# Fourteen single buffers for x1, planes kept on the chip, gates further ahead: a change to layer 1 of a four-layer kernel

## Chip, cores and metric

The kernel runs on one core of a Trainium2 chip. The metric is the device time of one execution in microseconds; of several runs the median is given. PE, ACT, DVE and POOL are the tensor, scalar, vector and GpSimd engines, SP the engine whose queue issues most transfers.

## What is computed

The input x has shape 256 x 256 x 128 (65,536 points of 128 channels, 33.6 MB in float32). Four layers follow each other, each x = x + layer(groupnorm(x)). Layer 0 is an attention over rows, layer 2 a triangle product like layer 1 but with 128 channels, layer 3 a small convolution. The change lies in layer 1 and in the first loads of layer 2. Layer 1 is:

```
xn = groupnorm(x)                                  # 32 groups, statistics over all points
a  = sigmoid((xn@Wa1 + ba1) * (xn@Wa2 + ba2))      # 16 channels
b  = sigmoid((xn@Wb1 + bb1) * (xn@Wb2 + bb2))      # 16 channels
g  = sigmoid(xn@Wg + bg)                           # 128 channels
z  = einsum('ikc,jkc->ijc', a, b)                  # 16 products of 256 x 256 matrices
x  = x + g * (layernorm_over_16_channels(z)@Wz + bz)
```

## The kernel before, in words

Between stages x lies in device memory with channels as rows: x1T after layer 0, x2T after layer 1. It is cut into NSC = 32 tiles of 128 channels x SC = 2048 points, 1 MB each, 8 KB per partition. The list order1 (L769) takes the tiles as 0, 16, 1, 17, and so on. Each engine and each transfer queue runs its instructions in the order in which the code lists them (manual_schedule); a transfer issued by SP that has to wait holds up all that SP issues after it. On-chip memory is handed out as a stack of pools; a pool has named buffers, bufs of each name, used in turn, so that the first writer of a new tile waits for all users of the old one. Where one pool is closed and another opened, the new one takes the addresses of the old.

**Before layer 1.** Layer 0 has three pools, one above the other: p2e (L481; the buffers p2_e, six of 8 KB per partition, and p2_es, five of 4 KB), p2c with the 8 KB tile triT, and p2 (p2_x, p2_rb and more). When they are closed, x1 is opened in their place: KEEP = 10 buffers of 8 KB (L772), and the first eight tiles are loaded by SP (load1, L775 to L781). A flag is then computed, and all engines branch on it (L795): a second, general attention follows only if the flag is set, which it isn't here. After the branch come the norm's factors (L198 to L209 and L818 to L829).

**Projections (L833 to L875).** Per tile, PE multiplies with two 128 x 32 weights (L859), ACT and DVE form the product (L868, L869), ACT the sigmoid into one of five p3_ab buffers (L842), and the four quarters of 64 KB go to abD, two through POOL and two through SP (store3, L848), one tile later. Of x, tiles 0 to 9 of the list stay in x1; the others pass through five more buffers (xs1, MORE = 5), tile i+5 being loaded when tile i is multiplied.

**Triangle product (L887 to L942).** For each of 16 channels, PE turns a matrix (L1822), ACT copies it out (L1824), PE multiplies (L1833), DVE subtracts plane 0 (L922) and sums (L928), ACT squares (L924) and POOL sums the squares (L929). Each plane is stored to znD at once (L933), not normalised. A pair of channels is loaded into one of three buffers z_A and z_B, and list positions 10 to 14 of x1 are loaded again on the way (L936). At the end DVE and ACT form the inverse deviation, 128 x 512 (L938 to L942).

**Gating (L947 to L1044).** For each position i of the list, in this order: PE and ACT make the gate of position i+LEAD (gate4; four matmuls in two halves, each through one of two PSUM buffers p4_pg, then a sigmoid into one of four buffers p4_g); SP fetches planes for four positions (fetch_z, each fourth i), and for every four positions PE spreads the inverse deviation over the rows through a p4_pg buffer and DVE multiplies the planes by it (scale_z, L969 and L972); PE multiplies the planes with Wz (L1014, p4_pz); DVE adds the bias and multiplies the gate, in place (L1022); POOL adds the result to x (L1033), or DVE does for the six positions in by_dve (L1029); ACT squares and sums the tile of i-1 for the next norm (sum4, L992), SP stores tile i-1 to x2T (L1039) and loads into a freed buffer (L1042). LEAD is 2. The first three gates are made ahead of the loop.

**Layer 2 opens (L1053 to L1186).** The norm's factors are computed from the sums, then seven tiles of x2T are loaded by SP (load5, L1103), the first four are squared (L1108) and summed by PE (L1124), and the main products (L1167) follow. Its buffers p5_x lie in the pool p5.

The profile shows names without layer and digits: x for the x1 tiles, p_ab, z_A, z_z, p_z (fetched planes), p_pg, p_g, p_pz, p_rb (spread deviation), p_junk (squares), p_x (p5_x in layer 2, p2_x in layer 0), p_e and p_es.

Of the kernel before, what the change touches and what calls it, by code (L numbers as in the profile page):

```python
# [16 lines left out]
P = 128  # L17
N = 256
# [14 lines left out]
def kernel(ctx: ExitStack, tc: tile.TileContext, a: dict, out: bass.AP):  # L33
# [734 lines left out]

    order1 = [b + h * NSC // 2 for b in range(NSC // 2) for h in range(2)]  # L769
    KEEP, MORE, FIRST = 10, 5, 8  # L770
    x1_scope = ExitStack()
    x1_pool = x1_scope.enter_context(tc.tile_pool(name="x1", bufs=KEEP))  # L772
    xs = {}

    def load1(i, pool):  # L775
        s = order1[i]
        xs[s] = pool.tile([P, SC], F32, name=f"x1_{s}", tag="x1")
        nc.sync.dma_start(xs[s], x1T[:, s * SC : (s + 1) * SC])

    for i in range(FIRST):  # L780
        load1(i, x1_pool)  # L781
# [51 lines left out]
    with x1_scope, tc.tile_pool(name="xs1", bufs=MORE) as xs_pool:  # L833
        with tc.tile_pool(name="p3", bufs=3) as sb, tc.tile_pool(
# [17 lines left out]
            for i in range(FIRST, KEEP + MORE):  # L852
                load1(i, x1_pool if i < KEEP else xs_pool)
            for i, s in enumerate(order1):
# [8 lines left out]
                if i >= KEEP and i + MORE < NSC:  # L863
                    load1(i + MORE, xs_pool)
# [12 lines left out]
        with tc.tile_pool(name="zc", bufs=1) as zc:  # L877
            s1 = zc.tile([P, 2 * N], F32, name="z_s1")

            spread = zc.tile([P, 16, 32], F32, name="spread")  # L880
            for h in range(2):
                nc.gpsimd.tensor_copy(
                    spread[:, :, 16 * h : 16 * h + 16],
                    sel[:, 16 * h : 16 * h + 16].unsqueeze(2).to_broadcast([P, 16, 16]),
                )

            with tc.tile_pool(name="z", bufs=2) as sb, tc.tile_pool(  # L887
                name="zps", bufs=3, space=PSUM
            ) as ps, tc.manual_schedule():
                s2 = sb.tile([P, 2 * N], F32, name="z_s2", bufs=1)  # L890
                base = sb.tile([P, 2 * N], F32, name="z_base", bufs=1)
                AB, stores = {}, []

                def load_z(g):
                    if g < 8:
                        AB[g] = [sb.tile([P, 2, 2 * N], F32, name=n, bufs=3) for n in ("z_A", "z_B")]
                        A, B = AB[g]
                        nc.sync.dma_start(A, abD[2 * g : 2 * g + 2, :].rearrange("c (p t) -> p c t", p=P))
                        for c in range(2):
                            nc.sync.dma_start(  # L900
                                B[:, c, :], abD[16 + 2 * g + c, :].rearrange("(q s t) -> s q t", q=4, t=CK)
                            )

                def turn_z(k):
                    if k < 16:
                        return tri_turn(nc, ps, sb, AB[k // 2][0], k % 2, ident, nc.scalar.copy)

                for g in range(3):
                    load_z(g)
                at = turn_z(0)  # L910
                for k in range(16):
                    if k and k % 2 == 0:
                        load_z(k // 2 + 2)
                    nxt = turn_z(k + 1)
                    pz = tri_multiply(nc, ps, at, AB[k // 2][1], k % 2).rearrange("p t n -> p (t n)")
                    at = nxt
                    Z = sb.tile([P, 2 * N], F32, name="z_z", bufs=4)
                    if k == 0:
                        nc.vector.tensor_copy(base, pz)
                        nc.vector.memset(Z, 0.0)  # L920
                    else:
                        nc.vector.tensor_tensor(Z, pz, base, ALU.subtract)  # L922
                        sq = s2 if k == 1 else sb.tile([P, 2 * N], F32, name="z_sq", bufs=3)
                        nc.scalar.activation(sq, Z, AF.Square)  # L924
                        if k == 1:
                            nc.vector.tensor_copy(s1, Z)
                        else:
                            nc.vector.tensor_tensor(s1, s1, Z, ALU.add)  # L928
                            (nc.vector if k == 15 else nc.gpsimd).tensor_tensor(s2, s2, sq, ALU.add)  # L929
                    stores.append((k, Z))  # L930
                    if len(stores) > 1 or k == 15:
                        for k_, Z_ in stores if k == 15 else stores[:1]:
                            nc.sync.dma_start(znD[k_].rearrange("(p t) -> p t", p=P), Z_)  # L933
                        stores = stores[1:]
                    if k % 2 == 1 and KEEP + k // 2 < KEEP + MORE:
                        load1(KEEP + k // 2, xs_pool)  # L936

                nc.vector.scalar_tensor_tensor(s1, s1, -1.0 / 16, s1, ALU.mult, ALU.mult)  # L938
                nc.vector.tensor_tensor(s2, s2, s1, ALU.add)
                nc.vector.tensor_scalar(s2, s2, 0.0, None, ALU.max)  # L940
                nc.scalar.activation(s2, s2, AF.Sqrt, bias=epst, scale=1.0 / 16)
                nc.vector.reciprocal(s1, s2)  # L942
# [4 lines left out]
            with tc.tile_pool(name="p4", bufs=3) as sb, tc.tile_pool(  # L947
                name="p4psg", bufs=2, space=PSUM
            ) as psg, tc.tile_pool(name="p4psz", bufs=2, space=PSUM) as psz, tc.manual_schedule():
                zs, gts, sums = {}, {}, []  # L950
                junk = sb.tile([P, SC], F32, name="p4_junk", bufs=1)
                by_dve = (5, 11, 17, 23, 29, NSC - 1)

                def fetch_z(i):
                    if i < NSC:
                        zs[i] = sb.tile([P, 2, CK], F32, name="p4_z")
                        for m in range(2):
                            nc.sync.dma_start(
                                zs[i][:, m, :],
                                znD.rearrange("k (j b t) -> b j k t", j=8, t=CK)[order1[i] + m],  # L960
                            )

                def scale_z(i):
                    if i < NSC:
                        rb = psg.tile([P, 2, CK], F32, name="p4_rb", tag="p4_pg")
                        for m in range(2):
                            for c in range(4):
                                q = slice(32 * c, 32 * c + 32)
                                nc.tensor.matmul(  # L969
                                    rb[q, m, :], lhsT=spread[q, order1[i] + m, :], rhs=s1[q, :], start=True, stop=True  # L970
                                )
                        nc.vector.tensor_tensor(zs[i], zs[i], rb, ALU.mult)  # L972

                def gate4(i):
                    if i < NSC:
                        xt = xs[order1[i]]
                        gts[i] = sb.tile([P, SC], F32, name="p4_g", bufs=4)
                        for h in range(2):
                            pg = psg.tile([P, 2, CK], F32, name="p4_pg")
                            for c in range(2):  # L980
                                k = 2 * h + c
                                nc.tensor.matmul(  # L982
                                    pg[:, c, :], lhsT=wgf, rhs=xt[:, k * CK : (k + 1) * CK], start=True, stop=True
                                )
                            nc.scalar.activation(
                                gts[i][:, h * 2 * CK : (h + 1) * 2 * CK], pg.rearrange("p c t -> p (c t)"),
                                AF.Sigmoid, bias=bgf,
                            )

                def sum4():  # L990
                    i = sums.pop(0)
                    nc.scalar.activation(  # L992
                        junk, xs[order1[i]], AF.Square, bias=c1neg, accum_out=qsum[:, i : i + 1]
                    )

                LEAD = 2
                fetch_z(0)
                fetch_z(4)
                for i in range(LEAD + 1):
                    gate4(i)  # L1000
                scale_z(0)
                for i, s in enumerate(order1):
                    xt = xs[s]
                    if i:
                        gate4(i + LEAD)
                    if i % 4 == 0:
                        fetch_z(i + 8)
                    if i % 4 == 2:
                        scale_z(i + 2)
# [25 lines left out]
                    if len(sums) > 1:  # L1035
                        sum4()
# [838 lines left out]
```

## Time and profile before

Three runs took 3423.06, 3427.47 and 3431.08 us; the profiled execution has a span of 3428.7 us.

| stretch of the profile | us from the start | length |
|---|---|---|
| layer 0 and before | 0 to 1481.7 | 1481.7 |
| first x1 loads, branch | 1481.7 to 1505.7 | 24.0 |
| norm factors, projections | 1505.7 to 1599.35 | 93.65 |
| triangle product, to the end of the reciprocal | 1599.35 to 1660.27 | 60.9 |
| gating, to its last add | 1660.27 to 1858.5 | 198.2 |
| layer 2 from its norm, layer 3 | 1858.5 to 3428.7 | 1570.2 |

Over the whole span PE is busy 92%, DVE 66%, ACT 59%, POOL 47%, and the x1 loads are 54 transfers of 1 MB. Such shares are means over stages with different limits, so a change in one stage has to be read in that stage: the table of windows gives busy times by stretch, the timeline what each instruction waited for ("[2.10 <-ACT p_g L985]" means that the engine stood idle for 2.10 us and that the sigmoid in L985 released it). A busy PE is not PE at its peak.

### The profile page before, as it was taken

To read this page: it belongs to the slowest core of one execution; us is meant where nothing else is said; L and a number is where in the kernel's file an instruction comes from. 1 tells how busy PE (TensorE), PEld (TensorE's weight loads), DVE (VectorE), ACT (ScalarE), POOL (GpSimd) and SP (SyncE) were. 2 spreads that over 40 slices of the span, in tenths; PEclk is the share of its full clock that TensorE was granted. 3 is DMA by queue.
4 is the path that set the end of the run, shared out by engine and by line. 5 is a ranking of instruction groups with operands and counts; after the bars stand their busy time and mean duration, and the time that the engine had idled before them with its cause. 6 is when DMAs were issued, how large, how long until landed. Compare 5 with 4: busy or idle time off the path is not lost.

```text
span 3428.7 us, 52984 instructions
## 1 busy us (share of the span) xinstructions
PE 3137.5 (92%) x20394; PEld 1652.5 (48%) x20394; DVE 2263.5 (66%) x2612; ACT 2015.2 (59%) x2204; POOL 1617.7 (47%) x928
## 2 busy tenths in 40 slices
PE   5769999999999999956896999999999999859998
PEld 5525555555555555513332444444899533324444
DVE  5627888888888888832454445544555677747876
ACT  3667777777777777623576444543444466736565
POOL 4146777777777777723364000000555344514443
PEclk8889999999999999979998999999999999969999
DMA  9882333333333333279595676856999899856764
GB/s 395 350 299 79 116 119 107 119 106 122 109 119 110 115 116 109 94 271 364 202 383 246 236 270 252 310 215 233 343 352 349 305 336 334 307 163 194 206 199 131
DMA packets 298860, 753.23 MB, mean 220 GB/s; under 512 B 75193, under 2 KB 145819, under 8 KB 249067
## 3 DMA queue, kind: packets, MB, share of 16 engines
q1 hardware_dynamic: 290571, 741.54, 59.8%
q0 software_dynamic: 7520, 6.67, 0.6%
q8 instruction: 163, 2.67, 0.3%
q10 hardware_dynamic: 512, 1.59, 0.1%
q14 instruction: 94, 0.77, 0.1%
HBM read 462.02 MB, written 287.66 MB: 219 GB/s over the span
## 4 chain that ended last, share of the span: by engine, by line
PE 42%; DMA 7%; POOL 2%; DVE 2%; issue 2%; ACT 1%; SPq 0%; ACTq 0%; POOLq 0%; DVEq 0%
PE p_pm L1167 13%; PE tp_z L1833 7%; PE p_pm L1320 6%; PE p_pm L1555 5%; PE tp_a L1822 2%; POOL x L1033 2%; DMA abD<-p_ab 2%; PE p_st L1124 1%; PE p_pt L1592 1%; DMA p_er<-eD 1%; PE p_eb L1081 1%; PE p_rz L1081 1%; DMA x<-x1T 1%; PE p_rk L1081 1%; PE p_pg L982 1%
## 5 line engine op out<-in xcount | busy, mean ns | idle before, releaser
L564 DVE TENSOR_TENSOR p_e<-p_S,triT 128x1024 f32<-128x1024 f32 x512 | 609.3, 1212 | 144.7 <-PE p_S L554 144.7
L574 POOL TENSOR_TENSOR p_es<-p_e 128x1024 f32<-128x1024 f32 x256 | 603.5, 2368 | 125.7 <-issue 66.1
L572 ACT ACTIVATE p_e<-p_e,mbT 128x1024 f32<-128x1024 f32 x512 | 552.0, 1138 | 61.4 <-DVE p_e L564 61.2
L1167 PE MATMUL p_pm<-p_zn,wf 128*128 128x512 f32 x1040 | 451.2, 596 | 1.4 <-DVE p_zn L1184 1.4
L539 PE MATMUL p_mm<-p_xn,w 128*128 128x512 f32 x768 | 405.0, 610 | 0.3 <-DVE p_v L534 0.3
L1167 PEld LDWEIGHTS p_pm<-p_zn,wf 128*128 128x128 f32 x1040 | 198.0, 191 | 255.4 <-issue 248.6
L554 PE MATMUL p_S<-p_q,p_k 32*128 32x256 f32 x4096 | 295.7, 401 | 3.5 <-DVE p_e L564 3.2
L554 PEld LDWEIGHTS p_S<-p_q,p_k 32*128 32x128 f32 x4096 | 186.2, 184 | 159.5 <-PE p_mm L530 91.7
L1569 POOL TENSOR_TENSOR p_q<-p_q,p_pb 128x2024 f32<-128x2024 f32 x32 | 144.1, 4502 | 250.9 <-DVE p_pb L1563 250.9
L1233 POOL DMA_DIRECT2D rs__18031<-rs2D x4 | 2.0, 500 | 533.2 <-PE p_pm L1167 533.2
L1833 PE MATMUL tp_z<-p_B,tp_at 128*128 128x256 f32 x1024 | 251.0, 388 | 2.6 <-DMA p_B<-bD 2.3
L587 PE MATMUL p_o<-p_e,p_v 128*32 128x256 f32 x4096 | 248.3, 383 | 0.0
L513 POOL TENSOR_TENSOR p_xn<-p_xn,p_rs 128x1024 f32<-128x1024 f32 x63 | 151.3, 2402 | 205.1 <-ACT p_xn L508 129.1
L1276 POOL TENSOR_TENSOR k<-k,p_sq 128x512 f32<-128x512 f32 x128 | 163.0, 1274 | 135.4 <-ACT p_sq L1274 135.4
L1386 POOL TENSOR_TENSOR p_x<-p_x,p_g 128x2048 f32<-128x2048 f32 x30 | 136.3, 4543 | 161.3 <-DVE p_g L1373 127.3
L1833 PEld LDWEIGHTS tp_z<-p_B,tp_at 128*128 128x128 f32 x1024 | 185.5, 191 | 25.5 <-issue 2.7
L539 PEld LDWEIGHTS p_mm<-p_xn,w 128*128 128x128 f32 x768 | 125.8, 190 | 104.4 <-issue 88.7
L1275 DVE TENSOR_TENSOR k<-tp_z,k 128x512 f32<-128x512 f32 x128 | 88.5, 692 | 129.4 <-ACT p_sq L1274 129.4
L587 PEld LDWEIGHTS p_o<-p_e,p_v 128*32 128x32 f32 x4096 | 120.2, 110 | 110.1 <-ACT p_g L545 41.5
L1272 ACT COPY p_K<-tp_z 128x512 f32<-128x512 f32 x128 | 75.0, 586 | 160.0 <-PE tp_z L1833 160.0
L545 ACT ACTIVATE p_g<-p_mm,bgh 128x512 f32<-128x512 f32 x128 | 88.0, 687 | 131.4 <-PE p_mm L539 131.3
L1200 DVE SCALAR_TENSOR_TENSOR p_b<-p_pm,b2w,p_b 128x1024 f32<-128x1024 f32 x64 | 82.1, 1284 | 125.0 <-PE p_pm L1167 110.6
(374 smaller groups left out, 5982.2 us busy)
## 6 DMA issues: line engine op xcount, KB each, us to landing
p_x<-x2T SPq DMA_DIRECT2D x64, 1024.0 KB
x<-x1T SPq DMA_DIRECT2D x54, 1024.0 KB
p_x<-in_x_dram SPq DMA_DIRECT2D x32, 1024.0 KB
p_x<-xT SPq DMA_DIRECT2D x64, 512.0 KB
x2T<-x SPq DMA_DIRECT2D x32, 1024.0 KB
aD<-p_a SPq DMA_DIRECT2D x32, 1024.0 KB
bD<-p_b SPq DMA_DIRECT2D x32, 1024.0 KB
p_A<-aD SPq DMA_DIRECT2D x32, 1024.0 KB
```

Of the source, the lines that this page charges most:

```text
L513: nc.gpsimd.tensor_tensor(xn, xn, groups[g]["rs"], ALU.mult)
L539: nc.tensor.matmul(pm, lhsT=w, rhs=t["xn"][:, cs_], start=True, stop=True)
L554: nc.tensor.matmul(Ss[h // 2][:, h % 2, u, :], lhsT=t["k"][hp, r * N + u * P : r * N + (u + 1) * P], rhs=t["q"][hp, r * N : (r + 1) * N], ...
L564: nc.vector.tensor_tensor(e[:, :, 2 * p : 2 * p + 2, :].rearrange("p u h n -> p h u n"), Ss[p], triT[:, 2 * p : 2 * p + 2, :, :], ALU.add,)
L572: nc.scalar.activation(e[:, u, :, :], e[:, u, :, :], AF.Exp, bias=mbT[:, u, i : i + 1])
L574: nc.gpsimd.tensor_tensor(es, e[:, 0, :, :], e[:, 1, :, :], ALU.add)
L587: nc.tensor.matmul(t["o"][hp, r % 2, :], lhsT=t["v"][:, r * 2 + u, hp], rhs=e[:, u, h, :], start=(u == 0), stop=(u == 1),)
L1167: nc.tensor.matmul(pm[:, c, :], lhsT=wf2[:, i, :], rhs=zns[s][:, k * CK : (k + 1) * CK], start=True, stop=True)
L1276: nc.gpsimd.tensor_tensor(k2, k2, sq, ALU.add)
L1320: nc.tensor.matmul(pm[:, c, :], lhsT=w, rhs=src[:, k * CK : (k + 1) * CK], start=True, stop=True)
L1555: nc.tensor.matmul(pm[:, 2 * c : 2 * c + 2, :], lhsT=w2c, rhs=src[:, r : r + 2, :], start=True, stop=True)
L1833: nc.tensor.matmul(pz[:, t, :], lhsT=at[:, u, t * P : (t + 1) * P], rhs=Bc[:, u, :], start=(u == 0), stop=(u == 1))
```

## The change

Line numbers in the text remain those of the kernel before. The change does this:

- x1 has fourteen pools of one 8 KB buffer each. In the projections tile i+14 of the list follows tile i in its buffer, so that positions 18 to 31 are left at the end. No x1 load is made in the triangle stage. The gating takes positions 24 to 31, 18 to 23 and then 0 to 17, and loads its own position j into the buffer of j-14: 18 loads instead of 17.
- The sixteen planes stay in one tile Z (32 KB per partition) in the pool z. After the reciprocal, DVE multiplies four planes at a time by the inverse deviation and SP stores them, 1 MB each. scale_z, spread and the stores inside the loop are gone. z_A and z_B have two buffers instead of three. In the steps ahead of the square root the same DVE operations stand in another order.
- LEAD is 4 instead of 2 and p4_g has five buffers instead of four; five gates are made ahead of the loop.
- The x tiles of layer 2 get a pool of their own, x5, opened ahead of p5 and so at lower addresses; the first four are loaded by POOL's queue.

```diff
-    KEEP, MORE, FIRST = 10, 5, 8
+    SLOTS, FIRST = 14, 8
...
-    x1_pool = x1_scope.enter_context(tc.tile_pool(name="x1", bufs=KEEP))
+    slots = [x1_scope.enter_context(tc.tile_pool(name=f"x1_{i}", bufs=1)) for i in range(SLOTS)]
...
-                if i >= KEEP and i + MORE < NSC:
-                    load1(i + MORE, xs_pool)
+                if i + SLOTS < NSC:
+                    load1(order1[i + SLOTS], i % SLOTS)
...
-                        AB[g] = [sb.tile([P, 2, 2 * N], F32, name=n, bufs=3) for n in ("z_A", "z_B")]
+                    AB[g] = A, B = [sb.tile([P, 2, 2 * N], F32, name=n) for n in ("z_A", "z_B")]
...
-                    if k % 2 == 1 and KEEP + k // 2 < KEEP + MORE:
-                        load1(KEEP + k // 2, xs_pool)
...
+            for q in range(4):
+                zq = Z[:, 4 * q : 4 * q + 4, :]
+                nc.vector.tensor_tensor(zq, zq, s1.unsqueeze(1).to_broadcast([P, 4, 2 * N]), ALU.mult)
+                nc.sync.dma_start(znD[4 * q : 4 * q + 4, :].rearrange("c (p t) -> p c t", p=P), zq)
...
+            order = [order1[i] for i in (*range(24, NSC), *range(18, 24), *range(18))]
...
-                        gts[i] = sb.tile([P, SC], F32, name="p4_g", bufs=4)
+                    gts[i] = sb.tile([P, SC], F32, name="p4_g", bufs=5)
...
-                LEAD = 2
+            LEAD = 4
...
-                    if i % 4 == 2:
-                        scale_z(i + 2)
...
-                    j = i - 3 + KEEP + MORE
+                j = i - 3 + SLOTS
...
-                        load1(j, x1_pool if j % (KEEP + MORE) < KEEP else xs_pool)
+                    load1(order[j], (j + 10) % SLOTS)
...
+    with tc.tile_pool(name="x5", bufs=7) as x5_pool, tc.tile_pool(name="p5", bufs=2) as sb, tc.tile_pool(name="p5psX", bufs=1, space=PSUM) as psX, tc.tile_pool(
-                xs[s] = sb.tile([P, SC], F32, name="p5_x", bufs=7)
-                nc.sync.dma_start(xs[s], x2T[:, s * SC : (s + 1) * SC])
+                xs[s] = x5_pool.tile([P, SC], F32, name="p5_x")
+                (nc.gpsimd if s < KB else nc.sync).dma_start(xs[s], x2T[:, s * SC : (s + 1) * SC])
```

## The prediction

> **What bounds the kernel now.** The change touches layer 1 and the first loads of layer 2. I read the table of windows first, cut where the stages of this part begin, then for each stage the timeline and the table of waits. Columns: stretch and its length, then busy time (and instructions) of PE, PEld, DVE, ACT and POOL, granted clock, DMA share, GB/s.
>
> ```profile
> 1464.00:1481.70 17.70, 7.51 (x12) 2.35 (x8) 12.03 (x16) 0.00 (x0) 4.10 (x2) 0.64 0.24 90
> 1481.70:1505.70 24.00, 1.12 (x4) 1.01 (x4) 0.81 (x6) 0.04 (x1) 0.00 (x0) 0.50 0.87 352
> 1505.70:1599.35 93.65, 63.68 (x532) 17.66 (x532) 25.56 (x41) 40.74 (x67) 31.57 (x64) 0.94 0.92 359
> 1599.35:1652.03 52.68, 42.71 (x192) 35.44 (x192) 20.29 (x30) 16.97 (x30) 16.14 (x15) 0.84 0.89 331
> 1652.03:1660.27 8.24, 3.71 (x9) 1.44 (x8) 7.25 (x7) 2.63 (x3) 1.09 (x1) 1.00 0.14 55
> 1660.27:1675.30 15.03, 11.04 (x32) 4.18 (x33) 1.22 (x1) 7.86 (x7) 0.00 (x0) 0.77 0.30 105
> 1675.30:1858.50 183.20, 161.84 (x600) 56.91 (x600) 101.62 (x148) 123.79 (x119) 117.67 (x26) 0.96 0.72 285
> ```
>
> Row 1: the tail of layer 0, DMA nearly idle. Row 2: nothing but the first eight x1 loads. Row 3, the projections: DMA. Row 4, the triangle product: DMA and PE by turns. Row 5: DVE's square root and reciprocal. Rows 6 and 7, the gating: no engine is full (PE 88%), so a chain sets the pace.
>
> Why row 2 is empty, from the waits of SP's queue and the timeline:
>
> ```profile
> SPq L778 <- DVE stats L638: 7.8, 1, 7.8
> ...
> 1463.50 0.64 PE L597 MATMUL p_z<-p_es,hot 128*32 128x256 f32 x8 [1.34 <-POOL p_es L574]
> ...
> 1505.66 1.28 ACT L207 ACT_TABLE_LOAD   x1 [44.70 <-SPq L795]
> ```
>
> The first x1 load writes what had been a p_e buffer, last used in 1464.1, yet waits for DVE's last reading of p_x, another pool. A pool here waits for every tile of each closed pool it overlaps. Behind the branch (L795) all wait for SP, and SP for the eight loads, until 1505.7.
>
> The gating, from the timeline (start, length, engine, line, what it had waited for):
>
> ```profile
> 1660.41 1.28 ACT L985 ACT_TABLE_LOAD   x1 [3.53 <-DVE z_s L942]
> ...
> 1686.88 3.05 PE L969 MATMUL p_rb<-z_s,spread 32*32 32x512 f32 x16 [2.10 <-ACT p_g L985]
> ...
> 1701.91 3.70 PE L982 MATMUL p_pg<-x,wgf 128*128 128x512 f32 x8 [0.99 <-ACT p_g L985]
> ...
> 1703.62 4.53 POOL L1033 TENSOR_TENSOR x<-x,p_g 128x2048 f32<-128x2048 f32 x1 [0.20 <-DVE p_g L1022]
> ```
>
> The first sigmoid waits for the last reader of the z pool (rule of pools again). The same matmuls took 3.05 after a wait of 2.10 and 1.92 at 1711.33 after one of 1.02: PE starts at half clock after a long wait.
>
> [...] waits of 2.10, 2.46 and 3.17 already brought it, waits up to 1.8 did not. [...]
>
> **The change part by part**, against the profiled span of 3428.7 (the three timed runs have a median of 3427.5). R is the end of the reciprocal, i a position of the gating loop.
>
> (1) *Fourteen single slots; projections.* Slots 0 to 7 take the first 64 KB above layer 0's small pool; the p2e pool (six 8 KB and five 4 KB buffers, 68 KB) lay there and was free at 1464.1. So the eight loads start then, not at 1481.7, and the branch opens when flag and loads are there, about 1491 (estimate: PE left the branch at 1489.8). From then the stage is DMA-bound: 32 tiles of 1.049 MB, 15 stores of 0.262 ahead of the last load, and 1.6 MB of layer 0's tail (17.7 us by 90 GB/s) are 39.1 MB; at 424 GB/s (the windows 1494 to 1500 had 423 and 426) 92.2 us, from 1466 (2 of latency) to 1558.3. I add 4 because SP's loads must follow layer 0's last small transfers through its queue (none to 14: the last x1T store landed at 1481.7). But a store now stands behind the load 17 tiles on, before it was 8: with five p_ab buffers the closing of tile m+5 waits for it, so 12 tiles are left after the last load, 12 x 1.75 (PE's 8 projection matmuls) = 21.0, and 3.3 from the last p_ab to the next stage, as now. End 1586.8 instead of 1599.35: **-12.5** (-20 to -6). Loads fall from 54 to 50; the five removed lie in the next stage, the one added in the gating.
>
> (2) *Triangle stage.* Five x1 loads and 16 plane stores go. PE repeats every 2.20 when nothing is late (1612 to 1618). The second multiply began 10.1 after the start; 13 x 2.20 to the fifteenth and 3.72 for the last two give 42.4 against 52.68: **-10.3** (-6 to -11). Two z_B buffers instead of three: a group's 1 MB is issued 4.9 before its use and lands in about 3.6, so it stays hidden. Row 5's DVE steps are the same ones in another order: 0. The memset of plane 0 lies ahead of the first multiply: 0.
>
> (3) *Planes normalised behind the last; start of the gating.* Four DVE multiplies 128x2048 at 2.29 and four 1 MB stores, each behind its multiply. 4.19 MB at some 360 GB/s (abD's 2 KB rows had 361 and 373) are 11.6; first issue R+2.6, landing 1.7: the last lands at R+15.9. Planes and gate buffers share an address range, so the first sigmoid waits for this store; behind it in ACT's queue stand all gates, and PE for PSUM. Then 1.28 table, 1.05 to PE's next half gate, four gates of 3.63 and 1.9 for the cold clock: first p_pz at R+34.6; now R+15.0: **+19.6** (+4 to +21; the low end if only the fetch of planes waited). Spread, scale_z and their eight p_z multiplies vanish.
>
> (4) *Pace of the gating.* Now scale_z costs eight times 1.92 of PE and a PSUM slot: stretches of six positions with two of them took 36 to 38, with one 32.5. Without it PE would need 3.63 + 1.07 = 4.70 per position. But gate i+4 goes into one of five buffers, and the fifth before it is gate i-1, which POOL reads until its add ends. With LEAD 2 and four buffers the same wait was for i-2. So a loop closes: POOL ends i-1, ACT +0.06 and 1.05, PE gate i+5 3.63 and p_pz of i+1, from its start to POOL 3.85, POOL's add 4.53: 13.12 for **two** positions. The by_dve positions are all odd and don't cut the even loop. From the first p_pz: 13 x 13.12 = 170.6 to that of i=26, then 8.4 and three POOL adds at 4.7 for 27, 28 and 30: 193.1. Each turn leaves PE idle 13.12 - 9.40 = 3.7, long enough for the slow restart, which cost 1.3 to 1.7 in the three cases above; part of it falls off the loop. I take 0.8 a turn, 10.4 in all (0 to 22): 203.5 against 183.2: **+20.3** (+10 to +32). DMA has room: 52 MB in 200 us.
>
> (5) *x2 lowest, four loads on POOL.* They lie under slots whose stores ended five positions earlier, so they start with POOL's last add, not at 1863.76. POOL's queue holds nothing else; SP keeps three. The first square moves from 10.2 to about 6.5 after the last add (then the factor of the norm binds), the fourth from 18.8 to about 13.3 (4 MB beside the last store): **-5.5** (-2 to -8).
>
> Sum: -12.5 - 10.3 + 19.6 + 20.3 - 5.5 = +11.6, 3440 in the span; in timed runs **3438**.
>
> **The rivals.**
> A, *the gate loop does not close*: it decides only if POOL's add has ended before ACT comes to the next sigmoid. For it: POOL is busy 64% of row 7. Against: the add ends 8.4 after p_pz, PE's round is 4.7. Then PE paces: 27 x 4.70 and some 25 for the last adds, 152 instead of 203.5, ending faster: 3388.
> B, *planes don't hold the gates*: the sigmoids follow the reciprocal, p_pz the fetch (R+19), 15.5 less: 3423. Against: two waits above show whole pools waiting.
> C, *the clock stays up* in the gating: 10.4 less, 3428. For it: no half clock in the steady part of row 7 now; its waits were under 2.
> D, *the slots don't start early*, that is, the new pools wait for all of layer 0: part (1) comes to 0, 3451.
>
> **How the numbers follow.** Forecast 0.42, A 0.12, B 0.14, C 0.18, D 0.14. Range 3412 to 3456: C and B with each other below, D above with 5 more; A is left out. A measurement of this kernel tells about 0.2% from no change, 7 us. Faster than 3420.6: A, half of B and a little of C: 0.24. Within: rest of B, most of C, the low quarter of the forecast: 0.30. Slower: 0.46.
>
> **What would show it.** x1 loads from about 1465; projections ending near 1587 with stores alone at the end; triangle stage without DMA waits; first p_pz 34 after the reciprocal; p_pz starts in pairs 4.7 and 8.5 to 9.8 apart with ACT's sigmoids waiting for POOL; slow restarts of PE there; p_x loads ahead of the last x2T store. Even spacing near 4.7 or sigmoids before the plane stores land would make it wrong.

## The result: slower by 1.6 per cent, and where the time went

The changed kernel takes 3485.11 us (median of four runs, 3475.49 to 3486.95), the kernel before, on the same chip, 3429.01 (four runs, 3423.06 to 3431.08). The ratio is 1.0161, 95% interval 1.0138 to 1.0184: 56 us more, where 3438 had been predicted with a range up to 3456.

From here on line numbers are those of the changed kernel unless a run is built on the kernel before: L964 is the gate's matmul, L967 its sigmoid, L993 p_pz, L1001 DVE's product, L1012 POOL's add, L1018 and L1023 the stores to x2T, L1082 the loads of x2, L1087 the squares, L1093 the store of rs2D.

The profiled execution has a span of 3473.8. Its table of windows, cut at the same events as that of before (length, then PE, PEld, DVE, ACT, POOL busy, granted clock, of which 1 is full speed, DMA share, GB/s):

```profile
1460.87:1493.12 32.25, 6.32 (x10) 2.35 (x10) 12.53 (x20) 0.00 (x1) 3.85 (x2) 0.65 0.82 311
1493.12:1587.26 94.14, 64.47 (x534) 20.94 (x534) 25.72 (x42) 40.84 (x67) 31.57 (x64) 0.92 0.92 358
1587.26:1630.00 42.74, 38.10 (x192) 33.44 (x192) 20.27 (x30) 16.84 (x30) 15.27 (x12) 0.89 0.60 197
...
1638.88:1672.56 33.68, 16.75 (x33) 7.08 (x33) 8.90 (x5) 11.19 (x10) 0.00 (x0) 0.66 0.47 172
1672.56:1900.46 227.90, 170.02 (x473) 62.44 (x472) 95.19 (x144) 119.47 (x115) 119.36 (x30) 0.81 0.64 236
1900.46:1937.23 36.77, 12.75 (x72) 4.17 (x72) 6.62 (x16) 18.46 (x14) 0.00 (x1) 0.59 0.57 237
```

In row 1 DMA is now 82% busy; before, it was at 24% until the first x1 load was issued. Row 3, the triangle, is at 60% DMA instead of 89%. Row 5, the gating, is the surprise: 227.9 instead of 183.2, with a granted clock of 0.81 instead of 0.96, so that PE is busy longer (170.0 instead of 161.8) with fewer matmuls (473 instead of 600). Row 6, the opening of layer 2 up to the store of rs2D, took 28.2 before.

The same kernel's timeline (start, length, engine, line; in brackets what the engine had waited for) at the seams ahead of the gating:

```profile
1467.49 1.88 ACTq L618 DMA_DIRECT2D p_rb<-rzD  x4
1477.42 2.34 POOL L626 TENSOR_TENSOR p_u<-p_u,p_rb 128x1024 f32<-128x1024 f32 x1 [15.04 <-DMA p_rb<-rzD]
1493.12 1.28 ACT L207 ACT_TABLE_LOAD   x1 [35.53 <-SPq L795]
...
1653.35 1.28 ACT L967 ACT_TABLE_LOAD   x1 [17.85 <-DMA znD<-z_Z]
...
1672.56 1.14 PE L993 MATMUL p_pz<-p_z,wz 32*128 32x512 f32 x8
```

The reader is to see three things: layer 0's last small load, p_rb, now goes beside x1 loads, and POOL waits 15.04 for it; the first sigmoid waits for the last plane store, as predicted; and the first p_pz comes 33.7 after the end of the reciprocal (1638.88). In the kernel before, POOL's wait for p_rb was 6.22:

```profile
1471.98 2.34 POOL L626 TENSOR_TENSOR p_u<-p_u,p_rb 128x1024 f32<-128x1024 f32 x1 [6.22 <-DMA p_rb<-rzD]
```

Now two turns of the gating (a turn is two positions, one round of the predicted loop):

```profile
1742.35 2.12 ACT L967 ACTIVATE p_g<-p_pg,bgf 128x1024 f32<-128x1024 f32 x2 [5.16 <-POOL x L1012]
...
1743.52 5.34 PE L964 MATMUL p_pg<-x,wgf 128*128 128x512 f32 x8 [3.68 <-ACT p_g L967]
...
1748.78 1.14 PE L993 MATMUL p_pz<-p_z,wz 32*128 32x512 f32 x8
...
1752.61 4.50 POOL L1012 TENSOR_TENSOR x<-x,p_g 128x2048 f32<-128x2048 f32 x1 [5.58 <-DVE p_g L1001]
...
1757.14 2.12 ACT L967 ACTIVATE p_g<-p_pg,bgf 128x1024 f32<-128x1024 f32 x2 [5.16 <-POOL x L1012]
...
1758.31 6.46 PE L964 MATMUL p_pg<-x,wgf 128*128 128x512 f32 x8 [3.69 <-ACT p_g L967]
...
1764.71 1.14 PE L993 MATMUL p_pz<-p_z,wz 32*128 32x512 f32 x8
```

The predicted loop is there step for step: the sigmoid waits for POOL's add, PE for the sigmoid (3.68 idle), POOL's next add comes 3.83 after p_pz. But the gate inside it takes 5.3 from its start to p_pz in one turn and 6.4 in the next, not 3.63. From one even add to the next it is 14.8, then 15.9, through all thirteen turns.

Last, the opening of layer 2 in the same timeline:

```profile
1884.77 0.56 POOL L1082 DMA_DIRECT2D p_x<-x2T  x1 [4.67 <-ACT p_junk L974]
...
1894.30 1.62 POOL L1082 DMA_DIRECT2D p_x<-x2T  x3
...
1895.40 2.24 SPq L1082 DMA_DIRECT2D p_x<-x2T  x2
...
1900.49 0.32 SPq L1018 DMA_DIRECT2D x2T<-x  x1
...
1900.85 0.89 SPq L1023 DMA_DIRECT2D x2T<-x  x1
...
1908.34 1.93 PE L1103 MATMUL p_st<-p_x,slide 128*32 128x512 f32 x8 [0.30 <-DVE off L1051]
...
1919.69 8.05 ACT L1087 ACTIVATE p_sq<-p_x,mr2neg,gn_rstd 128x2048 f32<-128x2048 f32 x4 [13.37 <-DMA x2T<-x]
```

Six x2 loads are issued ahead of the last two stores, although the code lists them behind (L1082 after L1018 and L1023). So these queues do not keep the order of the code across the seam between the gating's block and layer 2's; what orders them there stays open. The first square does not wait for its load, since PE reads x2's first tile at 1908.34. The profile puts the square's wait down to the last store. By the rule of pools this fits: p_sq lies in the pool p5, above x5, where the last gating tiles lay. That store goes out beside the loads and lands 19 after the last add. In the kernel before, the first square waited for its load and came 10.3 after the last add (1858.44):

```profile
1868.71 2.09 ACT L1108 ACTIVATE p_sq<-p_x,mr2neg,gn_rstd 128x2048 f32<-128x2048 f32 x1 [5.62 <-DMA p_x<-x2T]
```

Lengths of the stages in all traces (R is the end of the reciprocal; for kernels built on the one before the first column starts at a later first load, 17.6 after the pool was free, so 117.6 there compares as 135.2):

| kernel | first x1 load to first z_A | z_A to R | R to p_pz | p_pz to last add | last add to rs2D |
|---|---|---|---|---|---|
| before | 117.6 (135.2) | 60.9 | 15.0 | 183.1 | 28.2 |
| predicted | 122.7 | 50.6 | 34.6 | 203.5 | 22.7 |
| changed | 126.4 | 51.6 | 33.7 | 227.9 | 36.8 |
| e1, LEAD 3 | 126.7 | 50.4 | 28.9 | 167.7 | 35.4 |
| e2, filler reading x | 127.8 | 51.5 | 32.8 | 304.9 | 22.2 |
| e3, x2 loads on SP | 127.3 | 49.7 | 33.7 | 226.4 | 28.5 |
| e4, part (5) undone | 125.8 | 52.2 | 33.6 | 226.4 | 28.4 |
| e5, filler of four | 126.3 | 52.0 | 33.0 | 219.9 | 34.8 |
| e6, LEAD 2, part (5) undone | 126.9 | 49.8 | 26.9 | 163.3 | 28.3 |
| e7, before with part (5) | 117.4 | 59.3 | 14.7 | 183.1 | 35.7 |
| e8, four early loads | 133.4 | 51.3 | 33.6 | 227.8 | 36.8 |
| e9, filler of two | 126.8 | 49.8 | 33.7 | 208.9 | 32.3 |
| e10, before with three gate buffers | 116.7 | 60.3 | 15.7 | 245.3 | 28.2 |

Layer 0, which nothing here touches, freed its pool between 1459 and 1471 in these traces, so stages are compared by their lengths and not by their place.

### The profile page after: what moved, and what is told of

Its sections match the earlier page's. It is cut to its first block, busy times and chain, and to the rows that moved or that the text cites. A ratio compares the mean times of both kernels' runs of the same rounds, so it can differ in the third digit from the quotient of the medians.

```text
span 3473.8 us, 52672 instructions
## 1 busy us (share of the span) xinstructions
PE 3140.8 (90%) x20266; PEld 1661.4 (48%) x20266; DVE 2264.5 (65%) x2608; ACT 2014.6 (58%) x2204; POOL 1618.0 (47%) x930
## 4 chain that ended last, share of the span: by engine, by line
PE 42%; DMA 3%; DVE 2%; ACT 2%; POOL 2%; issue 1%; SPq 0%; ACTq 0%; POOLq 0%; DVEq 0%
PE p_pm L1146 13%; PE tp_z L1812 7%; PE p_pm L1299 6%; PE p_pm L1534 5%; PE p_pg L964 3%; POOL x L1012 2%; PE tp_a L1801 2%; PE p_st L1103 1%; PE p_pt L1571 1%; PE p_rz L1060 1%; PE p_eb L1060 1%; PE p_rk L1060 1%; DMA p_er<-eD 1%; ACT p_g L967 1%; PE p_pp L1427 1%
## 5 line engine op out<-in xcount | busy, mean ns | idle before, releaser
L964 PE MATMUL p_pg<-x,wgf 128*128 128x512 f32 x256 | 148.2, 735 | 70.1 <-ACT p_g L967 69.3
L1812 PEld LDWEIGHTS tp_z<-p_B,tp_at 128*128 128x128 f32 x1024 | 185.5, 191 | 22.2 <-DVE tp_at L1803 1.4
L1012 POOL TENSOR_TENSOR x<-x,p_g 128x2048 f32<-128x2048 f32 x26 | 117.2, 4510 | 145.0 <-DVE p_g L1001 144.7
L539 PEld LDWEIGHTS p_mm<-p_xn,w 128*128 128x128 f32 x768 | 126.7, 192 | 105.4 <-issue 89.7
```

Of the source, the lines that this page charges most:

```text
L539: nc.tensor.matmul(pm, lhsT=w, rhs=t["xn"][:, cs_], start=True, stop=True)
L964: nc.tensor.matmul(pg[:, c, :], lhsT=wgf, rhs=xt[:, k * CK : (k + 1) * CK], start=True, stop=True)
L1012: nc.gpsimd.tensor_tensor(xt, xt, gt, ALU.add)
L1812: nc.tensor.matmul(pz[:, t, :], lhsT=at[:, u, t * P : (t + 1) * P], rhs=Bc[:, u, :], start=(u == 0), stop=(u == 1))
```

## The experiments

Two questions were open: what makes the gating 24 longer than predicted, and why part (5) costs time instead of saving it. The times are medians; each ratio is to the kernel before on the same chip, run beside it. Its median there lay between 3428.4 and 3433.1, so times of different experiments compare to some 5 us; lengths of stages come from one trace each.

**e1, the distance to the buffer.** One edit:

```diff
-            LEAD = 4
+            LEAD = 3
```

> The changed kernel with LEAD 3 in place of 4 (five gate buffers kept, so gate i+3 goes into the buffer of i-2, not of i-1). Theory, the gate loop: the sigmoids no longer wait for POOL's add of the odd position before, PE paces at about 4.7 a position with no slow restarts, and from the first p_pz to the last add it takes about 152 (150 to 168) instead of 227.9; the first p_pz comes one gate earlier, about R+30. Time about 3410 (3400 to 3428). Rival, something else sets the pace (POOL's own adds, or the DMA of x1 and x2): 15 for two positions stays, time 3475 to 3487.

Measured 3419.07 (20 runs), ratio 0.9955 (0.9942 to 0.9967). PE's timeline in this run:

```profile
1743.13 1.14 PE L993 MATMUL p_pz<-p_z,wz 32*128 32x512 f32 x8
1744.20 3.70 PE L964 MATMUL p_pg<-x,wgf 128*128 128x512 f32 x8
1747.83 1.14 PE L993 MATMUL p_pz<-p_z,wz 32*128 32x512 f32 x8
1749.27 3.27 PE L964 MATMUL p_pg<-x,wgf 128*128 128x512 f32 x7 [0.30 <-ACT p_g L967]
```

p_pz follows p_pz by 4.7, no long wait, no slow gate. One gate less ahead takes the median 66 us under that of the changed kernel: the loop set the pace. The stage took 167.7, at the upper end of what was expected.

**e10, the same loop in the kernel before.** With LEAD 2 kept, one buffer less puts gate i+2 into the buffer of i-1:

```diff
-                        gts[i] = sb.tile([P, SC], F32, name="p4_g", bufs=4)
+                        gts[i] = sb.tile([P, SC], F32, name="p4_g", bufs=3)
```

> The kernel before with three gate buffers instead of four, its LEAD 2 kept: gate i+2 then goes into the buffer of i-1. Theory, the pace is set by which position's add frees the buffer, not by how many gates are ahead: the same loop of two positions as in the changed kernel, 14.8 to 15.9 for two where no planes are scaled, and from the first p_pz to the last add 225 to 255 instead of 183; the time 3475 to 3505. Rival, the loop needs five gates ahead (the PSUM and the queue of ACT being further ahead): the pace stays within 10 of 183, 3430 to 3443.

Measured 3489.34, ratio 1.0168 (1.0149 to 1.0188); the stage took 245.3. From its timeline (lines of the kernel before):

```profile
1746.91 2.12 ACT L985 ACTIVATE p_g<-p_pg,bgf 128x1024 f32<-128x1024 f32 x2 [5.16 <-POOL x L1033]
...
1748.08 5.20 PE L982 MATMUL p_pg<-x,wgf 128*128 128x512 f32 x8 [3.69 <-ACT p_g L985]
```

The waits of the changed kernel return, 5.16 and 3.69, and with them a slow gate. What counts is buffers minus lead: 4 - 2 and 5 - 3 leave two positions between a gate and the add that frees its buffer, 5 - 4 and 3 - 2 leave one.

**e2, e5 and e9, the clock inside the loop.** Extra matmuls behind the odd p_pz that POOL adds, results unused, to fill PE's idle time (the filler; h runs over the two p4_pz slots):

```diff
+                if i % 2 and i not in by_dve:
+                    for h in range(2):
+                        pj = psz.tile([P, 2, CK], F32, name="p4_pz")
+                        for c in range(2):
+                            nc.tensor.matmul(pj[:, c, :], lhsT=wgf, rhs=xt[:, c * CK : (c + 1) * CK], start=True, stop=True)
```

> The changed kernel with four more matmuls 128x512 (1.7 at full clock, results unused) into p4_pz slots behind the p_pz of the odd positions that POOL adds (1, 3, 7, 9, 13, 15, 19, 21, 25, 27). Theory, the loop of 13.12 with PE restarting at half clock after idling 3.7: in the nine turns with filler the gate takes 3.63 instead of 5.26 to 6.39 and the turn 13.1 instead of 14.8 to 15.9, so about 20 less (16 to 24): 3465. Rival, the clock is not the reason for the long gates (the loads and stores beside them, or the wait itself): turns stay at 14.8 to 15.9, 3480 to 3492.

Measured 3564.45, ratio 1.0349 (1.0278 to 1.042). This filler changed more than the clock: it read the x that POOL was still adding to, and so put a second wait for POOL into the loop, as PE's timeline shows:

```profile
1718.88 5.29 PE L1017 MATMUL p_pz<-x,wgf 128*128 128x512 f32 x8 [7.24 <-POOL x L1012]
1724.01 3.60 PE L964 MATMUL p_pg<-x,wgf 128*128 128x512 f32 x8
```

It still points to the clock: the slow matmuls were now the filler's, and the gate behind it took 3.60. (Some 30 us of its extra time lie behind the gating, in layers 2 and 3; that was not followed up.) In e5 the filler reads the next position's x, `rhs=xs[order[i + 1]][...]`:

> As the run with the four extra matmuls behind the odd p_pz, but reading x of the next position, which POOL has not added to yet, so that the filler waits only for DVE's reading of p_pz. Theory, the clock: PE idles under 2 ahead of the held-up gate, that gate takes 3.63 instead of 5.26 to 6.39, and each of the nine turns with filler 13.1 instead of 14.8 to 15.9: about 20 less than the changed kernel (14 to 24), 3465. Rival, the gates are long because of what runs beside them (loads, stores) or because of the wait itself: the turns stay at 14.8 to 15.9, 3480 to 3492.

Measured 3485.53 in four runs spread from 3467.78 to 3508.51, ratio 1.0168 (1.0113 to 1.0222); the time is no evidence either way. In the profiled execution, the lowest of the four, the gates behind filler took 3.53, but began 1.3 after the sigmoid had made room, since four matmuls take 3.53 and not the 1.7 that I had put down. The turn was 14.36. e9 halves the filler (`for h in range(1)`):

> As the last run with filler, with two matmuls instead of four (1.9, into the first p4_pz slot alone), so that they end before the held-up sigmoid lets PE go on. In the run with four the gate behind the filler took 3.53 instead of 5.26 to 6.39, but began 1.3 after the sigmoid had freed its PSUM slot, and the turn was 14.36. Theory, the clock: the gate again takes 3.53 to 3.63 and starts at once, the turn is 13.0 to 13.2 in the nine turns with filler; from the first p_pz to the last add about 208 (204 to 212) instead of 227.9, the time about 3466. Rival, two matmuls are too few to hold the clock: the gate takes 5 to 6.4 again and the turns stay at 14.8 to 15.9.

Measured 3454.9 (3453.09 to 3458.54), ratio 1.0074 (1.0057 to 1.0091), and 208.9 for the stage. PE's timeline:

```profile
1729.34 1.14 PE L993 MATMUL p_pz<-p_z,wz 32*128 32x512 f32 x8
1731.93 1.98 PE L1017 MATMUL p_pz<-x,wgf 128*128 128x512 f32 x4 [1.45 <-DVE p_g L1001]
1734.15 3.70 PE L964 MATMUL p_pg<-x,wgf 128*128 128x512 f32 x8 [0.23 <-ACT p_g L967]
1737.78 1.14 PE L993 MATMUL p_pz<-p_z,wz 32*128 32x512 f32 x8
```

The stretch between two drops of the clock, each in a turn without filler (columns as in the table of windows):

```profile
1710.42:1747.96 37.54, 30.49 (x101) 11.02 (x100) 16.71 (x26) 21.30 (x21) 22.59 (x5) 1.00 0.86 323
```

The clock stays full for 37.5 us. The gate takes 3.63 from start to p_pz and the turn 13.17 (adds at 1728.43 and 1741.60), the 13.12 of the prediction. More work on PE made the kernel some 30 us faster than the changed one, of which 19 lie in the gating: the idle stretches are what made the gates slow.

**e3 and e4, part (5) in the changed kernel.** e3 issues all x2 loads from SP; e4 also puts p5_x back into the pool p5.

```diff
-                (nc.gpsimd if s < KB else nc.sync).dma_start(xs[s], x2T[:, s * SC : (s + 1) * SC])
+                nc.sync.dma_start(xs[s], x2T[:, s * SC : (s + 1) * SC])
```

> The changed kernel with all x2 loads on SP (x2's pool still lowest). Theory, loads issued ahead of the last x2T stores take the bandwidth, and the p_sq buffers wait for the last of these stores: with three loads ahead instead of six the first square starts some 10 after the last add (now 19.2), and the adds of positions 27 to 30 are no longer behind loads in POOL's queue (3 less): together 10 to 16 less, about 3473. Rival, the queue makes no difference because the same bytes have to move before the squares: 0 to 3 less.

> The changed kernel with part (5) undone: p5_x back in the pool p5, its loads on SP, so that they follow the last store. From the last add to the store of rs2D 28.2 as before the change instead of 36.8, and POOL's last adds 3 earlier: 11 to 12 less, about 3474. Rival, the slow opening comes from the cold clock or from other causes outside part (5): no more than 3 less.

Measured 3472.35 for e3, ratio 1.0104 (1.0046 to 1.0163), and 3476.25 for e4, 1.0109 (1.0051 to 1.0167). These medians are 13 and 9 under that of the changed kernel, but both intervals just take in its ratio, 1.0161, so the times alone don't settle it. The traces do for the stage: the opening is 28.5 and 28.4, that of before, instead of 36.8. SP's queue in e3:

```profile
1899.25 0.46 SPq L1082 DMA_DIRECT2D p_x<-x2T  x1
1900.04 0.66 SPq L1023 DMA_DIRECT2D x2T<-x  x1
1900.74 3.26 SPq L1082 DMA_DIRECT2D p_x<-x2T  x4
```

Three loads ahead of the last store and four behind it are no better than seven behind it. The adds of the last positions ended 1.5 earlier without loads in POOL's queue, less than the 3 expected.

**e7, part (5) alone in the kernel before** (the three lines of the change for x5, nothing else):

> The kernel before with part (5) alone: x2's pool lowest, four loads on POOL, three on SP. Here the loads stand behind the last add in POOL's queue and behind the last store in SP's. Theory, part (5) goes wrong only because loads got ahead of the last stores, on which the p_sq buffers wait: here the loads start some 5 earlier and the last store goes out beside them, the first square comes 8 to 11 after the last add as now, the fourth 14 to 15 instead of 18.8, so rs2D is stored about 4 earlier: 4 less than before (0 to 6). Rival, any load beside the last store delays the first square by as much as it wins: 0, or up to 5 more.

Measured 3436.61 (14 runs), ratio 1.0003 (0.9982 to 1.0024). The rival was right: no gain. From the timeline (lines of before):

```profile
1856.74 1.27 SPq L1103 DMA_DIRECT2D p_x<-x2T  x3
...
1857.25 2.14 POOL L1103 DMA_DIRECT2D p_x<-x2T  x4 [6.93 <-DMA x2T<-x]
...
1867.49 2.09 ACT L1108 ACTIVATE p_sq<-p_x,mr2neg,gn_rstd 128x2048 f32<-128x2048 f32 x1 [11.31 <-DMA p_x<-x2T]
```

Here the loads still waited for the last store, so nothing started earlier. And the first square, 16.0 after the last add instead of 10.3, waited for its load: tile 0, on POOL's queue, was issued at 1857.25, tiles 4 to 6 on SP's from 1856.74 on, and tile 0 landed 10.1 after its issue. In the kernel before, the square came 5.0 after the issue of that load (1863.76 to 1868.71). That the loads on SP's queue held tile 0 up is an estimate from these two traces. In the trace the opening is 7.5 longer; the medians of the runs differ by 3.5 and the interval of the ratio takes in 1, so the size for the whole kernel stays open.

**e8, fewer early x1 loads.** `FIRST = 4` instead of 8:

> The changed kernel with four x1 loads instead of eight ahead of the flag; the other ten of the slots follow the branch. Theory A, part (1) as predicted: the projections are bound by DMA bytes, so what isn't loaded beside layer 0's tail is loaded later; p_rb of the last group waits 7 to 10 instead of 15.0 and the branch opens about 6 earlier, but DMA idles some 12 ahead of it: from the first x1 load to the first load of z_A 132 to 138 instead of 126.4, the time 6 to 12 more. Theory B, the delay of layer 0's last small transfers behind the x1 loads costs more than the early loads bring: 120 to 126, the time up to 6 less.

Measured 3492.84, ratio 1.016 (1.0114 to 1.0206): that of the changed kernel, so the time shows neither loss nor gain. From the first x1 load to z_A the trace has 133.4, against 125.8 to 127.8 in the eight traces with eight early loads. Its windows ahead of the branch:

```profile
1478.00:1488.00 10.00, 2.41 (x3) 1.17 (x4) 0.30 (x1) 0.00 (x0) 2.34 (x1) 0.50 0.46 152
1488.00:1500.00 12.00, 2.49 (x6) 1.00 (x4) 4.63 (x17) 1.28 (x1) 0.00 (x0) 0.64 0.33 111
```

DMA is more than half idle for 22 us (152 and 111 GB/s), and the stage is 7 longer: it is bound by bytes, as predicted, and in the stage early loads are worth having. Two parts of the expectation missed: p_rb still waited 15.06 with half as many loads, and the branch opened only 3 earlier (29.3 instead of 32.2 after the first x1 load), not 6.

**e6, what the runs pointed to.** The changed kernel with LEAD 2, five gate buffers, and e4's edit:

> The changed kernel with LEAD 2 (five gate buffers, gate i+2 goes into the buffer of i-3) and x2's loads back on SP in the pool p5, behind the last store. From the run with LEAD 3 (3419): the opening of layer 2 is 28.4 instead of 35.4, the last adds some 1.5 to 3 earlier, and one gate less (3.6) ahead of the first p_pz: 12 less, 3407 (3400 to 3414), faster than both kernels. Rival, with a lead of two gates the loop is again tight (or DMA sets the pace): the pace from first p_pz to last add is longer than the 167.7 of LEAD 3 by 10 or more, 3415 to 3430.

Measured 3406.84 (seven runs, 3403.85 to 3409.44), ratio 0.9917 (0.9888 to 0.9946): faster than both kernels. The window of its gating:

```profile
1665.96:1829.24 163.28, 148.07 (x489) 54.35 (x488) 93.52 (x141) 123.50 (x120) 117.75 (x26) 0.97 0.84 326
```

Against row 5 of the changed kernel the clock is 0.97 instead of 0.81 and PE is busy 91% of the stage instead of 75%.

## Why the prediction missed

The sign was right, the size not: 3438 against 3485. (The sum's +11.6 on the median of 3427.5 gives 3439, not 3438, and the terms of part (1) end at 1586.6, not 1586.8; neither matters here.) Two steps failed: the term for the slow restart in part (4) was too small, and part (5) had its sign wrong. By the sum's own terms, in the profiled execution:

1. **Part (1)**, -12.5 predicted. From the moment the pool was free, 126.4 instead of 135.2: **-8.8**. Slots, byte-bound stage and the end with stores alone were right. So were the 2 of latency put down: the first load was issued at 1460.87, and between 1463 and 1464 DMA moved 426 GB/s. The estimate that failed is the branch at "about 1491", with DMA running through but for the 4 added. Layer 0 ended 3.2 earlier here, so 1487.8 would compare with it. But p_rb waited 15.04, the branch opened at 1493.1 on ACT and at 1495.9 on PE, and SP's other loads stood behind it. From 1489 to 1494 DMA moved next to nothing (busy share 0.03, 8 GB/s). These 5 idle against the 4 allowed are only part of the 3.7 that is missing; where the rest lies stays open.
2. **Part (2)**, -10.3 predicted, **-9.3** measured.
3. **Part (3)**, +19.6 predicted, **+18.6** measured; the sigmoid's wait of 17.85 for the plane store is the one described, over at R+14.5 where 15.9 had been put down. The 2.29 for a DVE multiply of 128x2048 was an estimate, since the profile before has no such multiply; here the four took 2.28 to 2.29. Rivals B and D fall here and at the first x1 load (1460.87).
4. **Part (4)**, +20.3 predicted, **+44.7** measured. The loop of 13.12 was right (13.17 in e9, where the clock holds), so rival A falls. The term that was mis-sized is "I take 0.8 a turn" for the slow restart, because "part of it falls off the loop". Nothing falls off: the whole gate lies on the loop, and it grew by 1.6 and 2.8 in turn, 2.2 a turn on average. From the first p_pz to that of position 26 it took 199.2, 18.2 over the predicted 170.6 + 10.4. So the term came to 28.6 (199.2 less 170.6) instead of 10.4, and even my high end, 22 in all, was below it. It was drawn from three restarts after waits of 2.10 to 3.17 (granted clock 0.50 behind each), none as long as the 3.7 that I had worked out for the loop. Rival C, the clock staying up, is refuted (0.81 in the stage). The other 6.2 lie behind position 26, where the trace shows p_pz at half clock (0.50 from 1880 to 1895.3, behind a wait of 1.45), position 29 standing ahead of 30 in DVE's queue, and x2 loads in POOL's queue; only the last was sized (1.5 by e3 and e4).
5. **Part (5)**, -5.5 predicted, **+8.6** measured. The step that failed is "They lie under slots whose stores ended five positions earlier, so they start with POOL's last add". The loads did start early, ahead of the last stores; I had looked only at who waits for the loads, not at who waits for those stores. p_sq does: the first square came 19.2 after the last add, not about 6.5. "POOL's queue holds nothing else" was wrong too: the loads stood between the adds of 26 and 30. In e2, whose gating is so slow that POOL's loads were issued over 20 before the last add, the first square came 6.4 after that add and rs2D 22.2, the 6.5 and 22.7 predicted. So the estimate held only where the loads don't run beside the last stores.

Together -8.8 - 9.3 + 18.6 + 44.7 + 8.6 = +53.8, against +11.6. In the profiled execution 5.5 of it is missing behind rs2D (1536.6 instead of 1542.1). That part is unchanged and lies between 1536.6 and 1544.9 in the other traces but e2's, so I take it for spread. With layer 0 ending 3.2 earlier (1460.9 against 1464.1), the 53.8 leave the 45.1 between the two spans. The medians are 56 apart: the profiled execution is the fastest of its four, and no trace shows where the slower ones lose the rest. What delays p_rb, which waits as long beside four loads as beside eight, stays open too. The traces show only where: its load is issued 4.9 after the small store that it reads back, 1.8 before the change, and lands 9.9 later instead of 4.2.

## What to carry to other kernels

Making more ahead does not loosen a pipeline; buffers minus lead does. Count which instruction frees the buffer that the furthest product goes into, and follow that loop once around. If it leaves PE idle for some 3.7 us in each turn, price what PE does behind the wait at half clock until the clock comes back (3.3 to 5.6 us of PE's time here), and count all of the loss, since the slow work lies on the very loop that is waiting. Before moving loads to the front, list what waits for the stores that they overtake.

## What had not been expected of the hardware

The clock of the two turns shown above, read in the changed kernel's trace: what was granted while each gate was slow (1743.44 to 1746.85, and 1757.09 to 1763.92), and in the 3.4 us ahead of each (columns as in the table of windows):

```profile
1740.03:1743.44 3.41, 0.00 (x0) 0.00 (x0) 2.41 (x4) 1.09 (x2) 3.21 (x2) 1.00 0.33 139
1743.44:1746.85 3.41, 3.33 (x4) 1.51 (x5) 0.00 (x0) 3.01 (x4) 3.41 (x1) 0.50 1.02 329
...
1753.68:1757.09 3.41, 0.95 (x8) 0.12 (x5) 2.37 (x3) 0.00 (x0) 3.41 (x1) 1.00 0.05 22
1757.09:1760.51 3.42, 2.20 (x3) 1.17 (x4) 2.39 (x4) 3.37 (x3) 0.02 (x1) 0.50 0.84 275
1760.51:1763.92 3.41, 3.41 (x5) 1.34 (x5) 0.00 (x0) 1.84 (x3) 0.00 (x0) 0.50 1.06 279
```

- **Half clock that comes back every turn.** With PE idle 3.68 once per turn and busy for the rest, the clock dropped to 0.50 in each turn. The half clock of 1757.09 did not follow an idle stretch alone: in the 3.41 ahead of it PE was busy 0.95. After 3.42 in which PE was busy 2.20 the clock was still 0.50 (1760.51 to 1763.92); after the 3.33 of 1743.44 and the 3.41 of 1760.51 it was 1.00 again, for 10.24 each time. Over idle stretches of 1.45 and 0.23, with two matmuls between them, it stayed at 1.00 (e9).
- **Turns that alternate.** The turns were 14.8 and 15.9, by turns, all thirteen. In the two turns shown the half clock lasted 3.41 and 6.83. In the first of the turns shown PE works 3.33 at half clock, in the second 2.20 + 3.41 = 5.61; half of each is 1.7 and 2.8, and the two gates grew by 1.6 and 2.8. Why the loop settles into this rhythm no run tested.
